# Cross-attention weights divided in SBUF beside the self-attention cells, the second block's mask added there by GpSimd

## The chip, the cores and the metric

The kernel runs on one core of one Trainium2 chip. The metric is the device time of one launch in microseconds (us). The kernel before took 1626.58 us, the median of three runs from 1624.60 to 1629.66.

The engines are named as in the profile: PE (TensorE, matmuls; PEld its weight loads), DVE (VectorE), ACT (ScalarE), POOL (GpSimd), SP (SyncE, whose queue issues most DMAs). PE writes to PSUM, here eight banks of 128 x 512 floats; everything else lies in SBUF.

## What is computed

Two transformer blocks in sequence, all in float32, on `x` of 2 batches x 1024 rows x 256. Each has self-attention with 16 heads of 16, cross-attention to 64 context rows per batch, and a feed-forward. The first block's feed-forward is a mixture of 8 experts, of which each row takes two; the second's is one network. Only the second block's cross-attention has a mask over the context rows. Cut to what matters:

```python
# first block
q = _ln(latents);  x = latents + _mha(q, q, ...)          # self-attention
x = x + _mha(_ln(x), _ln(tokens), ...)                    # cross-attention, no mask
return _fuse_moe(x, ...)                                  # 8 experts, top 2
# second block
attn = softmax(einsum('bhnd,bhmd->bhnm', q, k) * SCALE);  x = x + (...)
q = _heads(layer_norm(x) @ q_w.T)
k = _heads(codebook_embeds @ k_w.T);  v = _heads(codebook_embeds @ v_w.T)
attn = einsum('bhnd,bhmd->bhnm', q, k) * SCALE
bias = (1.0 - mask)[:, None, None, :] * -10000.0
attn = softmax(attn + bias)
x = x + merge(einsum('bhnm,bhmd->bhnd', attn, v)) @ ca_proj_w.T
x = x + gelu(layer_norm(x) @ fc1_w.T + fc1_b) @ fc2_w.T + fc2_b
```

## The kernel before

**Cells.** Self-attention of one block is cut into 128 cells (loop at L959): 2 batches x 2 halves of the queries x 4 groups of 4 heads, times 8 parts of the keys. Eight cells are a head group `h`. A cell does two things. It takes the weights of its own part: four matmuls (L816), four Exp on ACT (L822), and later `product` (L858), which multiplies by the values (L867), copies on ACT (L876 or L879, into `part`) and adds on POOL (L880). And it looks ten cells ahead (`LEAD`) and takes row maxima: four matmuls (L805) and four reductions on DVE (L812). So in the last ten cells of a block, from cell 118 on, there are no maxima left; `maxima[0]` (L965) says whether there are. `helper()` (L314) is POOL while there are, DVE after. Once in eight cells, at cell 6 of a group, `largest` (L708) transposes the maxima (L713), which makes L713 a mark in the trace.

**Stream.** All other work of the block is a set of tasks, Python generators held in a `Stream` (L130). A task yields a positive cost in us when it has issued work, and a zero or negative number when it wants to wait: zero is one cell, -x is x us in cells of 2.9 us, one cell at least. After each cell the loop takes steps of tasks, most urgent and then highest rank first, until the allowance of the cell is used: 2.5 us a cell in the first block, 1.1 in the second, more where due times ask for it (`pace`, L161; L981). Steps without cost use no allowance. When the cells are over, `rest` (L178) issues what is left in order of rank, each task after its waits. All of this order is fixed when the program is made.

**Cross-attention** of a unit of 512 rows n (0 to 3, a batch half each) starts when the unit's self-attention is projected into `x` (`project`, L787). It is three tasks: a norm (`cnorm`), `weigh` (L1103) and `share` (L1273); the norm of unit n waits for the `weigh` of unit n-1, and `weigh` for the `share` of unit n-1. `weigh` works on 2 groups `g` x 4 rows of heads `r`, eight tiles of 128 x 512: query rows on partitions, and 8 stretches (4 query tiles x 2 heads) of 64 context rows along the free dimension. Its steps:

- `scores(g, n)` (L1128): for two tiles, four matmuls each (L1143); in the second block a matmul of one row before each of them puts the mask into the bank (L1134). While there are maxima ACT copies the banks to SBUF (L1154); otherwise `subtract` reads the bank.
- `largest(g, r)` (L1169): on a copied tile, DVE takes the maximum of each stretch (L1163) and POOL subtracts it (L1164).
- `weights_turned(g, n)` (L1173): four transposes on PE (L1179) per tile, and Exp on ACT out of PSUM (L1183) into `pt`.
- `product(g)` (L1189): four matmuls with the values (L1192), and sixteen with a table of ones, `picks` (L1202), that sum the weights; a copy on ACT (L1209), a reciprocal of the sums on DVE (L1211).
- `divided(g)` (L1214): four matmuls that spread the reciprocals over the rows (L1217) and a multiplication on DVE (L1224). For g = 1 it is in `share`, which then projects into `x` (L437).

While there are maxima these steps follow the list at L1232, eleven steps with at least a cell between most of them.

**The first block's end.** After the `share` of a unit, `dispatch_task` (L1306) routes it: norm, router matmuls, many small DVE operations, rows written to `sorted_rows`. `find` and `rows` (L1712, L1735) then say how many slots of 256 rows of one expert can start: after units 0 and 1 one slot, after unit 2 five (`NFULL`, L82). Slots (L1741) are issued only in `rest`. In the second block the feed-forward tasks (L1807) likewise start only in `rest`.

Of the kernel before, what the change touches and what calls it, by code (L numbers as in the profile page):

```python
# [41 lines left out]
F32 = mybir.dt.float32  # L42
# [3 lines left out]
ALU = mybir.AluOpType  # L46
# [4 lines left out]
P = 128  # L51
# [52 lines left out]
NCOL = 139  # L104


O_SUM, O_HEAD = 0, 128

O_ROWS, O_PART = 640, 704
NPICK = 768  # L110

W_O, W_V, W_Q, W_K = 0, 512, 1024, 1536
NSELF = 2048
# [88 lines left out]
def two_blocks(  # L202
# [323 lines left out]
    def self_attention(layer, tail, heads, arrive, extra, when_ready, beside=None):  # L526
# [224 lines left out]
        def side_by_side(parts, dst):  # L751

            i, o = bank()
            j, s = bank()
            for half, part in enumerate(parts):
                nc.tensor.matmul(
                    o[64 * half : 64 * (half + 1), :], lhsT=picks[:, O_ROWS : O_ROWS + 64],
                    rhs=part, start=True, stop=True,
                )
            for half, part in enumerate(parts):  # L760
                for c in range(4):
                    nc.tensor.matmul(
                        s[32 * c : 32 * (c + 1), :P],
                        lhsT=picks[:, O_PART + 32 * half : O_PART + 32 * (half + 1)],
                        rhs=part[:, c * P : (c + 1) * P],
                        start=(half == 0),
                        stop=(half == 1),
                    )
            inv = small.tile([P, P], F32, tag="inv", name=f"inv_{names}", bufs=1)
            nc.vector.reciprocal(inv, s[:, :P])  # L770
            nc.scalar.copy(dst, o)
            free.extend((j, i))
            yield 1.5
            yield -1.6
            i, by = bank()
            for c in range(4):
                nc.tensor.matmul(
                    by[:, c * P : (c + 1) * P],
                    lhsT=picks[:, O_HEAD + c * P : O_HEAD + (c + 1) * P],
                    rhs=inv, start=True, stop=True,  # L780
                )
            nc.vector.tensor_tensor(dst, dst, by, ALU.mult)
            free.append(i)
            yield 0.55
            yield -1.0
# [72 lines left out]
        def product(cells):  # L858

            h = cells[0] // 8  # L860
            b, g = h // 8, h % 4
            for cell in cells:
                stream.until(("values", b, cell % 8 & 6))
            n, o = bank()
            for cell in cells:
                for j in range(4):
                    nc.tensor.matmul(  # L867
                        o[32 * j : 32 * j + VW, :],
                        lhsT=V[b][:, cell % 8, 4 * g + j, :],
                        rhs=exps.pop((cell, j)),  # L870
                        start=(cell == cells[0]),
                        stop=(cell == cells[-1]),
                    )
            if cells[0] % 8 == 0:
                acc[h] = opool.tile([P, 512], F32, tag="acc", name=f"acc_{names}{h}")
                nc.scalar.copy(acc[h], o)  # L876
            else:
                part = opool.tile([P, 512], F32, tag="part", name=f"part_{names}{cells[0]}")
                nc.scalar.copy(part, o)  # L879
                helper().tensor_tensor(acc[h], acc[h], part, ALU.add)  # L880
            free.append(n)
            if cells[-1] % 8 == TB - 1:
                at_cell(cells[-1] + 3, lambda: finish(h, cells[-1] + 3))
# [219 lines left out]
    def weigh(layer, b, pool, w, name, held):  # L1103
# [21 lines left out]
        shape = [P, 4 * 2, SK]  # L1125
        less, pts, whole_scores = {}, {}, set()

        def scores(g, n):  # L1128

            got = [(r, *bank()) for r in (2 * n, 2 * n + 1)]  # L1130
            for t in range(4):
                for r, _, p in got if layer == 1 else ():
                    at = slice(32 * r, 32 * r + 1)
                    nc.tensor.matmul(  # L1134
                        p[:, t * P : (t + 1) * P].rearrange("p (u k) -> p u k", k=SK),
                        lhsT=ones[at, :],
                        rhs=mask_f[at, b * SK : (b + 1) * SK].unsqueeze(1).to_broadcast([1, 2, SK]),
                        start=True,
                        stop=False,
                    )  # L1140
                for r, _, p in got:
                    rows = slice(32 * r, 32 * r + 32)
                    nc.tensor.matmul(  # L1143
                        p[:, t * P : (t + 1) * P],
                        lhsT=q[rows, g, t * P : (t + 1) * P],
                        rhs=kbd[rows, g, b].rearrange("p u k -> p (u k)"),
                        start=(layer == 0),
                        stop=True,
                    )
            for r, i, p in got:  # L1150
                sc = less[g, r] = pool.tile([P, 512], F32, tag="sc", name=f"sc_{name}{g}{r}", bufs=4)
                if maxima[0]:

                    nc.scalar.copy(sc, p)  # L1154
                    whole_scores.add((g, r))
                else:
                    subtract(sc, p, nc.vector, f"{g}{r}")
                free.append(i)

        def subtract(sc, src, engine, tag):  # L1160
# [5 lines left out]
                mx.unsqueeze(2).to_broadcast(shape), ALU.subtract,  # L1166
            )

        def largest(g, r):  # L1169
            if (g, r) in whole_scores:  # L1170
                subtract(less[g, r], less[g, r], nc.gpsimd, f"{g}{r}")

        def weights_turned(g, n):  # L1173

            for r in (2 * n, 2 * n + 1):
                i, p = bank()
                sc = less.pop((g, r))
                for t in range(4):
                    nc.tensor.transpose(  # L1179
                        p[:, t * P : (t + 1) * P], sc[:, t * P : (t + 1) * P], ident  # L1180
                    )
                pt = pts[g, r] = pool.tile([P, 512], F32, tag="p1", name=f"pt_{name}{g}{r}", bufs=4)
                nc.scalar.activation(pt, p, AF.Exp, scale=SCALE)  # L1183
                free.append(i)


        inverse = {}

        def product(g):  # L1189
            i, o = bank()  # L1190
            for r in range(4):
                nc.tensor.matmul(  # L1192
# [7 lines left out]
            for r in range(4):  # L1200
                for c in range(4):
                    nc.tensor.matmul(  # L1202
                        s[32 * c : 32 * (c + 1), :P],
                        lhsT=picks[:, O_SUM + 32 * r : O_SUM + 32 * (r + 1)],
                        rhs=pts[g, r][:, c * P : (c + 1) * P],
                        start=(r == 0),
                        stop=(r == 3),
                    )
            nc.scalar.copy(q[:, g, :], o)  # L1209
            inv = inverse[g] = pool.tile([P, P], F32, tag="inv", name=f"inv_{name}{g}", bufs=2)  # L1210
            nc.vector.reciprocal(inv, s[:, :P])  # L1211
            free.extend((i, j))

        def divided(g):  # L1214
            i, p = bank()
            for c in range(4):
                nc.tensor.matmul(  # L1217
# [6 lines left out]
            nc.vector.tensor_tensor(q[:, g, :], q[:, g, :], p, ALU.mult)  # L1224
            free.append(i)

        held.update(ot=q, divided=divided)
        cost = 1.9 if layer else 1.0
        SC, LA, TU, PR, DI = scores, largest, weights_turned, product, divided
        if maxima[0]:  # L1230

            for now, wait in (  # L1232
                (((SC, 0, 0), (LA, 0, 0)), 0.0),
                (((LA, 0, 1),), 0.0),
                (((SC, 0, 1), (LA, 0, 2)), 0.0),
                (((TU, 0, 0), (LA, 0, 3)), 0.0),
                (((SC, 1, 0), (LA, 1, 0)), 0.0),
                (((TU, 0, 1), (LA, 1, 1)), 0.0),
                (((SC, 1, 1), (LA, 1, 2)), 0.0),
                (((PR, 0), (LA, 1, 3)), -1.5),  # L1240
                (((TU, 1, 0),), None),
                (((DI, 0), (TU, 1, 1)), -1.4),
                (((PR, 1),), None),
            ):
                for step, *args in now:
                    step(*args)
                us = sum({SC: cost, TU: 1.15, PR: 1.1, DI: 0.55}.get(step[0], 0.0) for step in now)
                if us:
                    yield us
                if maxima[0]:  # L1250
                    yield 0.0
                elif wait is not None:
                    yield wait
            return
        for step, *args, wait in (
            (SC, 0, 0, None),
# [1 line left out]
            (TU, 0, 0, None),  # L1258
            (SC, 1, 0, None),
            (TU, 0, 1, -1.3),  # L1260
            (PR, 0, None),
            (SC, 1, 1, None),
            (TU, 1, 0, None),
            (DI, 0, None),
            (TU, 1, 1, -1.6),
            (PR, 1, None),
        ):
            step(*args)
            yield {SC: cost, TU: 1.15, PR: 1.1, DI: 0.55}[step]
            if wait:  # L1270
                yield wait

    def share(w, name, first, held):  # L1273

        yield -2.6
        held["divided"](1)
        yield 0.55
        yield -1.2
        for t0 in range(0, 4, 2):
            yield from project_task(held["ot"], w, first + t0, t0, 2)  # L1280
# [732 lines left out]
def _layout(inputs):  # L2013
# [81 lines left out]
    cols[:E, C_RB] = l0["router_b"]  # L2095

    picks = np.zeros((P, NPICK), f32)
    for r in range(4):
        for u in range(2):
            for c in range(4):  # L2100
                picks[SK * u : SK * (u + 1), O_SUM + 32 * r + 8 * c + 2 * r + u] = 1.0
    for j in range(4):
        for d in range(DH):
            picks[32 * j + d, O_ROWS + DH * j + d] = 1.0
# [49 lines left out]
```

## Time and profile before

The profiled execution took 1611.58 us; its span on the core, from first to last instruction, is 1609.8 us at a mean granted PE clock of 0.988.

| what | number |
|---|---|
| median of the runs | 1626.58 us |
| profiled execution, span | 1611.58 us, 1609.8 us |
| cells of the first block, last matmul | to about 588 us |
| slots of the experts | 597 to about 941 us |
| cells of the second block, last matmul | to about 1451 us |
| last cross-attention projected | 1523 us |
| L1134, mask matmuls | 256 instructions, 27.5 us of PE busy |
| L1202 and L1217, sums and their spreading | 512 and 128 instructions, 17.5 and 17.6 us |
| POOL subtractions (L1164) | 38 of 64 tiles |

A matmul of float32 appears as two instructions, so 512 matmul records of L1202 are 8 units x 32 matmuls. Matmuls on different rows or columns of the array overlap in time, so busy times of a group are more than what it takes from the cells around it. A line of the groups reads: line, engine, operation, output from inputs, shape, count; then busy time in us and the mean of one in ns; then idle time just before and what ended it. A line of the timeline reads: start in us, length in us, engine, line, operation, count. A line of busy times reads: stretch, its length, then busy time and instructions of PE, PEld, DVE, ACT and POOL, the granted clock, the DMA share and GB/s.

### The profile page before, as it was taken

The numbers are of one execution on the slowest core, as the hardware profiler recorded it, in microseconds if no ns is written. First come the engines' busy times: TensorE is split into PE (matmuls) and PEld (weight loads), VectorE is DVE, ScalarE is ACT, GpSimd is POOL, SyncE is SP. The second block draws the span as 40 slices with busy tenths as digits, with TensorE's granted clock in tenths as the row PEclk, the third lists the DMA queues.
The fourth block names the chain that finished last, engine by engine and source line by source line (L and its number), as shares of the span: only waits on it lengthen the run. The fifth ranks groups of instructions, "written<-read, shape, count | busy, mean of one in ns | idle before, by whom it ended". The sixth has DMA issues, their size and how long they took to land. (4 is left out here: it accounts for less than half of the span.)

```text
span 1609.8 us, 28322 instructions
## 1 busy us (share of the span) xinstructions
PE 1574.8 (98%) x10710; PEld 876.0 (54%) x10710; DVE 982.6 (61%) x2094; ACT 914.7 (57%) x1770; POOL 410.9 (26%) x546
## 2 busy tenths in 40 slices
PE   7999999999999999999999999999999999999998
PEld 3433444444544447888888653344344445446766
DVE  5797766677679747511114458876777777854400
ACT  3487767666765665332223337876776676674321
POOL 2233423135235203311112033411222322311000
PEclk9899999999999999999999999999999999999999
DMA  5334311101000115386556320101010002000000
GB/s 158 114 134 169 138 27 31 28 25 47 15 21 34 54 50 196 105 278 205 187 188 216 92 78 23 35 21 24 31 38 17 22 14 84 20 9 21 14 13 26
DMA packets 55751, 121.07 MB, mean 75 GB/s; under 512 B 12218, under 2 KB 26428, under 8 KB 55228
## 3 DMA queue, kind: packets, MB, share of 16 engines
q1 hardware_dynamic: 51772, 109.07, 20.9%
q0 software_dynamic: 3456, 9.51, 1.6%
q8 instruction: 86, 1.41, 0.4%
q10 hardware_dynamic: 384, 0.66, 0.2%
q14 instruction: 53, 0.43, 0.1%
HBM read 71.68 MB, written 38.88 MB: 69 GB/s over the span
## 5 line engine op out<-in xcount | busy, mean ns | idle before, releaser
L812 DVE TENSOR_REDUCE mx_s<-banks 128x1 f32<-128x512 f32 x1024 | 634.0, 681 | 209.5 <-PE banks L805 207.2
L822 ACT ACTIVATE pt_s<-banks 128x512 f32<-128x512 f32 x1024 | 532.8, 609 | 157.1 <-PE banks L805 123.8
L805 PE MATMUL banks<-KS,QS 16*128 16x512 f32 x2048 | 535.1, 631 | 2.9 <-DVE count L1446 1.4
L816 PE MATMUL banks<-qb_s,KS 32*128 32x512 f32 x2048 | 516.8, 622 | 6.9 <-DVE qb_s L715 3.6
L880 POOL TENSOR_TENSOR acc_s<-acc_s,part_s 128x512 f32<-128x512 f32 x141 | 179.4, 1272 | 434.5 <-ACT part_s L879 433.9
L816 PEld LDWEIGHTS banks<-qb_s,KS 32*128 32x128 f32 x2048 | 180.8, 187 | 178.7 <-DVE mx_s L812 106.3
L867 PE MATMUL banks<-pt_s,v_s 128*20 128x512 f32 x2048 | 262.7, 604 | 1.5 <-DVE mx_s L812 1.0
L805 PEld LDWEIGHTS banks<-KS,QS 16*128 16x128 f32 x2048 | 200.3, 186 | 71.7 <-issue 34.2
L867 PEld LDWEIGHTS banks<-pt_s,v_s 128*20 128x20 f32 x2048 | 43.1, 98 | 185.8 <-ACT pt_s L822 130.4
L1686 PE MATMUL banks<-w_slot,h_s 128*128 128x256 f32 x640 | 143.1, 380 | 0.0
L1686 PEld LDWEIGHTS banks<-w_slot,h_s 128*128 128x128 f32 x640 | 120.6, 190 | 19.7 <-DVE mx_s L812 1.5
L879 ACT COPY part_s<-banks 128x512 f32<-128x512 f32 x155 | 92.7, 598 | 62.3 <-PE banks L867 52.6
L1695 DVE SCALAR_TENSOR_TENSOR ys<-banks,gate,b 128x256 f32<-128x256 f32 x40 | 19.3, 482 | 163.0 <-PE banks L1686 161.8
L1662 ACT ACTIVATE h_s<-banks,w_slot 128x256 f32<-128x256 f32 x104 | 43.7, 471 | 111.1 <-issue 64.0
L1656 PE MATMUL banks<-xsT,w_slot 128*128 128x256 f32 x416 | 95.4, 381 | 0.7 <-ACT xsT L376 0.7
L1701 POOL DMA_INDIRECT results<-ys,to x40 | 38.8, 970 | 223.0 <-DVE ys L1695 180.5
L1656 PEld LDWEIGHTS banks<-xsT,w_slot 128*128 128x128 f32 x416 | 77.4, 190 | 14.9 <-DVE mx_s L812 2.3
L1164 POOL TENSOR_TENSOR sc_c<-sc_c,mx_c 128x512 f32<-128x512 f32 x38 | 40.0, 1053 | 97.6 <-DVE mx_c L1163 97.5
L1819 ACT ACTIVATE h_f<-banks,w_ff 128x512 f32<-128x512 f32 x32 | 22.0, 687 | 73.9 <-PE banks L1816 73.9
L635 PE MATMUL banks<-xT_s,w_att 128*128 128x512 f32 x128 | 63.9, 635 | 0.0
L1828 PE MATMUL banks<-w_ff,h_f 128*128 128x256 f32 x256 | 57.3, 380 | 0.0
L1662 ACT ACTIVATE h_s<-banks,spare 128x256 f32<-128x256 f32 x56 | 23.4, 471 | 58.7 <-issue 30.4
(272 smaller groups left out, 1640.2 us busy)
## 6 DMA issues: line engine op xcount, KB each, us to landing
w_slot<-in_ff_w_dram SPq DMA_DIRECT2D x40, 576.0 KB
sorted_rows<-fill SPq DMA_DIRECT2D x36, 520.0 KB
w_slot<-in_ff_w_dram SPq DMA_DIRECT2D x26, 514.0 KB
whole<-acc_s SPq DMA_DIRECT2D x30, 256.0 KB
spare<-in_ff_w_dram SPq DMA_DIRECT2D x14, 514.0 KB
xs<-sorted_rows SPq DMA_DIRECT2D x20, 260.0 KB
y<-results SPq DMA_DIRECT2D x16, 256.0 KB
QS<-stq_s SPq DMA_DIRECT2D x124, 32.0 KB
```

The source lines that it names most:

```text
L635: nc.tensor.matmul(p, lhsT=w[:, at + k * D + pair * P : at + k * D + (pair + 1) * P], rhs=xT[b][:, k, blk * 512 : (blk + 1) * 512], start= ...
L805: nc.tensor.matmul(sc, lhsT=QS[h % 4][r, qc * P : (qc + 1) * P], rhs=K[r, kh * 512 : (kh + 1) * 512], start=True, stop=True,)
L812: return i, lambda: nc.vector.tensor_reduce(mx[h][:, qc, j, kh : kh + 1], sc, AX.X, ALU.max)
L816: nc.tensor.matmul(sc, lhsT=K[r, n * P : (n + 1) * P], rhs=QB[h][r, :], start=True, stop=True)
L822: nc.scalar.activation(pt, sc, AF.Exp, scale=SCALE)
L867: nc.tensor.matmul(o[32 * j : 32 * j + VW, :], lhsT=V[b][:, cell % 8, 4 * g + j, :], rhs=exps.pop((cell, j)), start=(cell == cells[0]), st ...
L879: nc.scalar.copy(part, o)
L880: helper().tensor_tensor(acc[h], acc[h], part, ALU.add)
L1656: nc.tensor.matmul(ph[:, n, :], lhsT=w[:, at : at + P], rhs=xT[:, k, :], start=(k == 0), stop=(k == 1),)
L1662: nc.scalar.activation(h1[:, f, :], ph[:, n, :], AF.Gelu, bias=w[:, W_B1 + f : W_B1 + f + 1])
L1686: nc.tensor.matmul(py, lhsT=h1[:, f, h * P : (h + 1) * P], rhs=w[:, f * D : (f + 1) * D], start=(f == 0), stop=(f == 7),)
L1828: nc.tensor.matmul(py[:, n, :], lhsT=h1[:, f, t * P : (t + 1) * P], rhs=w2[:, f * D : (f + 1) * D], start=(f == 0), stop=(f == 7),)
```

## The change

A `weigh` that starts while there are maxima (`whole`) no longer sums and divides after the product. It takes Exp in SBUF (`exponentials`), sums each stretch of 64 on DVE, takes 8 reciprocals per row and lets `helper()` multiply (`divided`); the turned tiles are then only copied by ACT, and `product` is the four matmuls and the copy. In the second block its scores have no mask matmuls: POOL adds the mask to the copied tiles (`mask`). The steps follow a computed list of 19 (first block) or 21 (second block) steps, one cell each at least. `share` then has no division and starts with its second wait. A `weigh` that starts without maxima keeps the old steps, renamed `undivided` and `division`. The planner's costs follow. The table for the sums becomes one window that is shifted, `inv` moves to the buffers of `xn`, and `part` has three buffers instead of two.

```diff
-                part = opool.tile([P, 512], F32, tag="part", name=f"part_{names}{cells[0]}")
+                part = opool.tile([P, 512], F32, tag="part", name=f"part_{names}{cells[0]}", bufs=3)
...
+        whole = maxima[0]
+
         def scores(g, n):
             got = [(r, *bank()) for r in (2 * n, 2 * n + 1)]
+            masked = layer == 1 and not maxima[0]
             for t in range(4):
-                for r, _, p in got if layer == 1 else ():
+                for r, _, p in got if masked else ():
...
-                        start=(layer == 0),
+                        start=not masked,
...
+        def mask(g, r):
+            if (g, r) in whole_scores:
+                sc = less[g, r].rearrange("p (c k) -> p c k", k=SK)
+                row = mask_f[:, b * SK : (b + 1) * SK].unsqueeze(1).to_broadcast(shape)
+                nc.gpsimd.tensor_tensor(sc, sc, row, ALU.add)
+
+        def exponentials(g, r):
+            nc.scalar.activation(less[g, r], less[g, r], AF.Exp, scale=SCALE)
+
+        def divided(g, r):
+            sc = less[g, r].rearrange("p (c k) -> p c k", k=SK)
+            sm = pool.tile([P, 8], F32, tag="smc", name=f"sm_{name}{g}{r}", bufs=4)
+            nc.vector.tensor_reduce(sm, sc, AX.X, ALU.add)
+            nc.vector.reciprocal(sm, sm)
+            helper().tensor_tensor(sc, sc, sm.unsqueeze(2).to_broadcast(shape), ALU.mult)
...
-                nc.scalar.activation(pt, p, AF.Exp, scale=SCALE)
+                if whole:
+                    nc.scalar.copy(pt, p)
+                else:
+                    nc.scalar.activation(pt, p, AF.Exp, scale=SCALE)
...
         def product(g):
...
+            nc.scalar.copy(q[:, g, :], o)
+            free.append(i)
+        def undivided(g):
...
-        def divided(g):
+        def division(g):
...
+        costs = {
+            scores: 1.9 if layer and not maxima[0] else 1.0, weights_turned: 1.15, product: 0.55,
+            undivided: 1.1, division: 0.55,
+        }
+        if whole:
+            m = layer
+            cells = [[] for _ in range(19 + 2 * m)]
+            for k in range(8):
+                g, r = divmod(k, 4)
+                at = k + (4 + m) * g
+                if r % 2 == 0:
+                    cells[at].append((SC, g, r // 2))
+                    cells[at + 7 + m].append((TU, g, r // 2))
+                if m:
+                    cells[at].append((MA, g, r))
+                cells[at + m].append((LA, g, r))
+                cells[at + m + 2].append((EX, g, r))
+                cells[at + m + 3].append((DI, g, r))
+            for g in range(2):
+                cells[11 + m + (7 + m) * g].append((PR, g))
+            for now in cells:
+                for step, *args in now:
+                    step(*args)
+                us = sum(costs.get(step, 0.0) for step, *_ in now)
+                if us:
+                    yield us
+                if now is not cells[-1]:
+                    yield 0.0 if maxima[0] else -1.5
...
     def share(w, name, first, held):
-        yield -2.6
-        held["divided"](1)
-        yield 0.55
+        if held["division"]:
+            yield -2.6
+            held["division"](1)
+            yield 0.55
         yield -1.2
```

More of the change, by code (lines that the diff above doesn't have):

```diff
@@ L104 @@
 NCOL = 139
-O_SUM, O_HEAD = 0, 128
-O_ROWS, O_PART = 640, 704
-NPICK = 768
+O_SUM, O_HEAD = 512, 0
+O_ROWS, O_PART = 552, 616
+NPICK = 680
 W_O, W_V, W_Q, W_K = 0, 512, 1024, 1536
@@ L768, in side_by_side @@
                     )
-            inv = small.tile([P, P], F32, tag="inv", name=f"inv_{names}", bufs=1)
+            inv = small.tile([P, D], F32, tag="xn", name=f"inv_{names}", bufs=6)[:, :P]
             nc.vector.reciprocal(inv, s[:, :P])
@@ L1182, in weights_turned, with product @@
                 pt = pts[g, r] = pool.tile([P, 512], F32, tag="p1", name=f"pt_{name}{g}{r}", bufs=4)
-                nc.scalar.activation(pt, p, AF.Exp, scale=SCALE)
+                if whole:
+                    nc.scalar.copy(pt, p)
+                else:
+                    nc.scalar.activation(pt, p, AF.Exp, scale=SCALE)
                 free.append(i)
+        def product(g):
+            i, o = bank()
+            for r in range(4):
+                nc.tensor.matmul(
+                    o[32 * r : 32 * (r + 1), :],
+                    lhsT=vbd[:, b, 4 * g + r, :],
+                    rhs=pts[g, r],
+                    start=True,
+                    stop=True,
+                )
+            nc.scalar.copy(q[:, g, :], o)
+            free.append(i)
         inverse = {}
-        def product(g):
+        def undivided(g):
             i, o = bank()
@@ L1203, in product @@
                         s[32 * c : 32 * (c + 1), :P],
-                        lhsT=picks[:, O_SUM + 32 * r : O_SUM + 32 * (r + 1)],
+                        lhsT=picks[:, O_SUM + 6 - 2 * r : O_SUM + 38 - 2 * r],
                         rhs=pts[g, r][:, c * P : (c + 1) * P],
@@ L1209, in product @@
             nc.scalar.copy(q[:, g, :], o)
-            inv = inverse[g] = pool.tile([P, P], F32, tag="inv", name=f"inv_{name}{g}", bufs=2)
+            inv = inverse[g] = small.tile([P, D], F32, tag="xn", name=f"inv_{name}{g}", bufs=6)[:, :P]
             nc.vector.reciprocal(inv, s[:, :P])
             free.extend((i, j))
-        def divided(g):
+        def division(g):
             i, p = bank()
@@ L1225, in divided @@
             free.append(i)
[L1227 to L1244, printed above, removed]
+        held.update(ot=q, division=None if whole else division)
+        costs = {
+            scores: 1.9 if layer and not maxima[0] else 1.0, weights_turned: 1.15, product: 0.55,
+            undivided: 1.1, division: 0.55,
+        }
+        SC, MA, LA, EX, DI, TU, PR = (
+            scores, mask, largest, exponentials, divided, weights_turned, product
+        )
+        if whole:
[15 more added lines that the diff above has]
+            for now in cells:
                 for step, *args in now:
                     step(*args)
-                us = sum({SC: cost, TU: 1.15, PR: 1.1, DI: 0.55}.get(step[0], 0.0) for step in now)
+                us = sum(costs.get(step, 0.0) for step, *_ in now)
                 if us:
                     yield us
[L1250 to L1253, printed above, removed]
+                if now is not cells[-1]:
+                    yield 0.0 if maxima[0] else -1.5
             return
@@ L1260, in weigh @@
             (TU, 0, 1, -1.3),
-            (PR, 0, None),
+            (undivided, 0, None),
             (SC, 1, 1, None),
             (TU, 1, 0, None),
-            (DI, 0, None),
+            (division, 0, None),
             (TU, 1, 1, -1.6),
-            (PR, 1, None),
+            (undivided, 1, None),
         ):
             step(*args)
-            yield {SC: cost, TU: 1.15, PR: 1.1, DI: 0.55}[step]
+            yield costs[step]
             if wait:
@@ L2097, in _layout @@
     picks = np.zeros((P, NPICK), f32)
[L2098 to L2101, printed above, removed]
+    for u in range(2):
+        for c in range(4):
+            picks[SK * u : SK * (u + 1), O_SUM + 6 + 8 * c + u] = 1.0
     for j in range(4):
```

## The prediction

> **What bounds the kernel now.** I read the page's busy times and slices first, then busy time by stretch, then the groups of instructions of the cross-attention, then the timeline.
>
> ```profile
> PE 1574.8 (98%) x10710; PEld 876.0 (54%) x10710; DVE 982.6 (61%) x2094; ACT 914.7 (57%) x1770; POOL 410.9 (26%) x546
> ...
> PE   7999999999999999999999999999999999999998
> ...
> DVE  5797766677679747511114458876777777854400
> ACT  3487767666765665332223337876776676674321
> ```
>
> PE is covered in nearly every slice, with DVE and ACT at six to eight tenths beside it in the two stretches of cells. The Trainium skill, page "Perfetto Trace Analysis", section "Identifying the Most-Contended Engine", warns that matmul busy time is a poor measure because matmuls are pipelined. So I tested PE by what a cell costs with and without other PE work. Busy times by stretch (sum, then each engine):
>
> ```profile
> 110.20:134.36 24.16, 24.16 (x200) 8.17 (x196) 21.91 (x40) 20.51 (x41) 9.09 (x19) 1.00 0.40 136
> 265.40:304.10 38.70, 38.70 (x325) 19.04 (x321) 25.83 (x43) 27.55 (x53) 10.34 (x10) 1.00 0.14 28
> 477.37:512.16 34.79, 32.87 (x228) 14.06 (x224) 28.49 (x75) 21.04 (x41) 11.85 (x22) 1.00 0.05 16
> 553.30:588.40 35.10, 34.93 (x313) 16.45 (x309) 15.62 (x32) 26.69 (x53) 1.04 (x1) 1.00 0.00 1
> 588.40:641.50 53.10, 49.68 (x363) 37.03 (x362) 38.21 (x147) 26.71 (x51) 12.71 (x13) 0.97 0.50 171
> ```
>
> The first two are eight cells each. Matmuls other than L805, L816 and L867 cover 0.7 us of the first and 14.7 us of the second (by the timeline): 14.5 us longer for 14.0 us of extra PE work. Over the 28 such stretches of both blocks a straight line gives 24.3 us + 1.06 x extra PE time; with DVE's and ACT's extra time added to the fit these cost 0.25 and 0.27 us per us. A bare cell is 3.0 us. PE sets the pace, but DVE is at 21.9 of 24.2 us even in bare cells. In the third stretch, full of the router's small DVE operations, DVE is at 28.5 of 34.8 and the cells are longer than their PE work: DVE is the next bound.
>
> **What the skill says.** "SBUF — State Buffer", section "Who interferes with whom": GpSimd shares a port pair with DVE; a DVE instruction with two SBUF inputs contends with a GpSimd instruction that reads SBUF, tensor_reduce never does. The trace agrees: L1357 (two SBUF inputs, usually 0.19 us) took 1.14 us beside a GpSimd add, while the reduces of L1163 stay at 0.63 to 0.69 us. The new DVE reduces and reciprocals are of the free kind, so the added GpSimd work slows only the router's and norms' small operations.
>
> **The change part by part.** The present prices, by shape, and pieces of the timeline (start, length):
>
> ```profile
> L1134 PE MATMUL banks<-mask_i,ones 1*128 1x128 f32 x256 | 27.5, 281 | 0.0
> L1202 PE MATMUL banks<-pt_c,picks 128*32 128x128 f32 x512 | 17.5, 273 | 0.0
> L1217 PE MATMUL banks<-inv_c,picks 128*128 128x128 f32 x128 | 17.6, 280 | 0.3 <-DVE inv_c L1211 0.2 <-DVE mx_s L812 0.2
> L1211 DVE RECIPROCAL inv_c<-banks 128x128 f32<-128x128 f32 x16 | 15.3, 958 | 25.3 <-PE banks L1202 25.3
> L1224 DVE TENSOR_TENSOR q_c<-q_c,banks 128x512 f32<-128x512 f32 x16 | 10.9, 682 | 12.8 <-PE banks L1217 12.8
> L1163 DVE TENSOR_REDUCE mx_c<-sc_c 128x8 f32<-128x512 f32 x38 | 25.6, 673 | 14.7 <-ACT sc_c L1154 14.7
> L1164 POOL TENSOR_TENSOR sc_c<-sc_c,mx_c 128x512 f32<-128x512 f32 x38 | 40.0, 1053 | 97.6 <-DVE mx_c L1163 97.5
> L1183 ACT ACTIVATE pt_c<-banks 128x512 f32<-128x512 f32 x64 | 35.6, 612 | 20.6 <-PE banks L1179 19.9 <-ACT pt_c L1183 0.6
> ```
> ```profile
> 258.13 1.05 PE L1143 MATMUL banks<-kbd,q_c 32*128 32x128 f32 x14
> 258.91 0.70 PE L805 MATMUL banks<-KS,QS 16*128 16x512 f32 x2
> ...
> 490.06 1.29 POOL L880 TENSOR_TENSOR acc_s<-acc_s,part_s 128x512 f32<-128x512 f32 x1 [10.51 <-ACT part_s L879]
> 490.27 1.14 DVE L1357 TENSOR_TENSOR hot_m<-hot_m,desc 128x32 f32<-128x32 f32 x1
> ...
> 1177.19 0.49 PE L1134 MATMUL banks<-mask_i,ones 1*128 1x128 f32 x3
> 1178.98 0.70 PE L805 MATMUL banks<-KS,QS 16*128 16x512 f32 x2
> ```
>
> Only tasks whose scores begin while maxima are still taken get the new form. By the scores' times these are three of the first block (scores from 258, 389 and 534 us; maxima end near 553) and two of the second (1177 and 1311; the third begins at 1431, after maxima end near 1415).
>
> PE, per task. One sums step runs from 295.8 to 296.8 (1.0 us), two are 2.0; one division step from 304.6 to 305.5 (0.9), two are 1.8. Gone: 3.8 us. In the second block scores with masks hold PE from 1177.19 to 1178.98 (1.8 us), those of the first from 258.13 to 258.91 (0.8): four steps give another 4.0, so 7.8. All five: 3 x 3.8 + 2 x 7.8 = 27.0 us. That is the whole possible gain.
>
> DVE, per task. Gone: 2 x 0.96 + 2 x 0.68 = 3.3. New: 8 sums at 0.67 (L1163's row) and 8 reciprocals of 128x8; the nearest rows are 0.18 (128x4, L1409) and 0.34 (128x32, L497), I take 0.2. 7.0 in all, net +3.7. ACT: 8 Exp more at about 0.6, net +4.8, as the copies after the turns cost what the Exp there cost (0.60 against 0.61). GpSimd: 8 multiplications at 1.05 = 8.4; in the second block 8 mask adds at 1.05 to 1.27 (L429, an add with the same broadcast), so 17 to 19. It is busy 10 of 39 us in such cells, and the third `part` buffer lets ACT run ahead of it.
>
> Give-back. The fit gives 3.7 x 0.25 + 4.8 x 0.27 = 2.2 us per task. The other bound is denser: maximum, sum and reciprocal come in cells where this task has no PE work, so four cells in a row hold 2.48 + 0.87 of DVE or more, one of them 2.48 + 1.55: 14.1 us of DVE against 11.8 for four bare cells. Twice per task that is 4.6, near 5 with ACT. I take 3; the ends are 2.2 and 5.
>
> New waits. Exp waits on ACT for GpSimd's subtraction two cells before, the sum on DVE for an Exp one cell before, the turns on PE for a multiplication three cells before; behind each stand the next cell's reductions, Exps and matmuls. With GpSimd at most two such operations and one add per cell (3.4 us of about 4) these hold, unless GpSimd stands before a DMA (it waited up to 11.2 us for `by_s` before L508). I count nothing, with 3 us per block as the bad end.
>
> First two tasks of the first block: 3.8 - 3 = 0.8 each, -1.6. They last 19 cells, not 11. Their successors wait for the projected self-attention rows anyway (481.7 us), so the chain isn't later, only the router's work beside it.
>
> Second block: 7.8 - 3 = 4.8 each, -9.6. The first task took 19 cells as its costs exceeded the allowance of 1.1 us a cell; 21 steps with 9.7 us of cost take some 22 to 25. The second ends 5 to 10 cells later, near cell 118, and the next starts in the tail. There 2.8 of 4 blocks of feed-forward remain when the last cross-attention ends (1523 us), so lateness is filled. I charge 1 us: -8.6.
>
> Third task of the first block. It starts at cell 113; its sixteenth step falls on cell 128, so two turns, a product and the projection (5.4 us of PE) pass the last cell. Before, its projection ran at 575.6, 12.8 us before the cells ended at 588.4. By the planner's costs and waits (1.15 + 1.5 + 0.55 + 1.2 + 4.0) it now ends about 9 us after, and the router's task behind it, which already ran its statistics in those cells, has 5.8 of waits more to its normalisation: 15.5 after the end instead of 3 (591.4), so 12.5 later. Slots 1 to 4 need the rows it sorts (two units guarantee 2 x 2 x 512 - 8 x 255 = 8 rows, one slot); their first matmul came at 641.5, 53.1 after the cells. Meanwhile PE has the other work, 45 to 59 us of it. The last twelve cells shrink by 3 us (PE loses 7, but ACT, at 26.7 of 35.1, gains 2.4); the fourth task's division and projection, which ran after 641.5, now come before (4.5). Sum: -3 + 12.5 - 4.5 = +5, between 0 and +15.
>
> Total: -1.6 - 8.6 + 5 = -5.2 us on the profiled run's 1611.6 (span 1609.8 and 1.8 around it): 1606.4, a ratio of 0.9968. The profiled run is 15 us below the median of 1626.58, so I apply the ratio: 1621.
>
> The moved tiles (`inv` among the six `xn`, `picks` 88 columns shorter) I cost at nothing: a reciprocal's tile is read within 8 us, and picks arrives long before use. If that cover went, a norm would wait 1 us or so.
>
> **Rivals.**
> Full gain: PE alone counts and the tail fills: -27.0, 1599.6. For it, the slope of 1.06; against it, DVE at nine tenths in bare cells. Chance 0.20.
> Late rows (slower): the third task ends 21 us later relative to the cells, the whole distance, and the router's DVE chain (37 us from 586 to 623) then meets the fourth task's maxima and subtractions (13 us of DVE), 5 more. The tail is -3 + 21 - 4.5 + 5 = +18.5, the total +8.3: 1635. It decides once slot 1's first matmul is over 76 us after the last cell. For it: slot 0 is the only slot at hand. Chance 0.27.
> DVE and ACT take PE's place: 5 us back per task: +2.4 - 5.6 + 1 + 5 = +2.8, 1629. Chance 0.10.
> The third task falls back to the old form, pushed past the end of maxima by the later router: the tail stays, -1.6 - 8.6 = -10.2, 1616. Chance 0.05.
> Forecast: 0.38, own range 1614 to 1629.
>
> **How the numbers follow.** What a measurement here can tell from no change is about 0.3%, 4.9 us. Faster: full gain 0.20, fallback 0.05, 0.22 of the forecast: 0.47. Same: 0.13 of the forecast and 0.08 of the fourth case: 0.21. Slower: late rows 0.27, 0.05 of the others: 0.32. The range, 1602 to 1636, takes in the unknown costs and most of the outer cases.
>
> **What would show it.** Right: L1134's count falls from 256 to 128, the sums' from 512 to 192; heads of the second block with a task 1.5 us shorter each; slot 1 about 65 us after the first block's last cell, with some 7 us of PE idle before it. Wrong: PE waiting in cells for ACT's new Exp or for DVE behind GpSimd; five tasks not in the new form; no idle before slot 1.

## The result and the profile after

Beside runs of the kernel before on the same chip (median 1628.1 us) the changed kernel took 1616.4 us, the median of four runs: a ratio of 0.9935, interval 0.9918 to 0.9953. A second measurement, on one of the three chips of the experiments, gave 1610.2 us and 0.9957 (0.9943 to 0.9971). The ratios and intervals are estimated from the single runs and are not the quotients of the medians (0.9928 and 0.9969 here). The forecast was 0.9968. So the kernel is 0.4 to 0.65% faster.

The profiled execution of after took 1614.6 us, 3 us more than that of before in the table above. The experiments' three chips ran the kernel before at 1612 to 1615 us (medians), where its first profile (1611.6) also lies, and not at 1626 to 1628. A different chip would explain this, but the record names none for the first measurement. Nor is it a common factor: before took 0.8 to 1.0% more there, after (1616.4 against 1610.2) only 0.4%. Times from different chips are compared below as ratios to the kernel before on the same chip, and checked against the stretches of the traces. A difference of two ratios is turned into us by 1612; its uncertainty is worked out from the two intervals.

The totals and slices of after, to hold against those of before:

```profile
PE 1560.5 (97%) x10182; PEld 853.7 (53%) x10182; DVE 1013.8 (63%) x2178; ACT 939.3 (58%) x1821; POOL 472.2 (29%) x589
...
PE   7999999999999888899999999999999999999998
...
DVE  5788776877878856511114458876777878845400
```

PE has 528 instructions fewer and is busy for 14.3 us less; DVE has 31 us more. New are the eights in PE's slices 14 to 17: holes about the end of the first block's cells and behind it. The groups of after by shape, new and shrunk ones:

```profile
L1139 PE MATMUL banks<-mask_i,ones 1*128 1x128 f32 x128 | 12.9, 282 | 0.0
L1240 PE MATMUL banks<-pt_c,picks 128*32 128x128 f32 x192 | 8.3, 280 | 3.1 <-issue 3.1
L1191 DVE TENSOR_REDUCE sm_c<-sc_c 128x8 f32<-128x512 f32 x40 | 26.8, 670 | 0.0
L1192 DVE RECIPROCAL sm_c<-sm_c 128x8 f32<-128x8 f32 x40 | 8.1, 203 | 1.4
L1185 ACT ACTIVATE sc_c<-sc_c 128x512 f32<-128x512 f32 x40 | 26.0, 651 | 0.0
L1193 POOL TENSOR_TENSOR sc_c<-sc_c,sm_c 128x512 f32<-128x512 f32 x33 | 34.9, 1057 | 13.9 <-DVE sm_c L1192 13.8
```

Forty tiles are five tasks: the change does what it says, at about the prices taken (0.67, 0.2, 0.65 and 1.06 us; 0.67, 0.2, 0.6 and 1.05 were forecast). GpSimd takes 33 of the 40 multiplications, DVE the seven that come after the maxima. The stretches that the prediction showed of before, here of after (stretch, length, then PE, PEld, DVE, ACT and POOL busy, clock, DMA share, GB/s):

```profile
110.20:134.70 24.50, 24.37 (x201) 8.37 (x197) 21.97 (x40) 20.52 (x41) 9.06 (x19) 1.00 0.43 143
260.05:293.91 33.86, 33.86 (x252) 14.36 (x249) 25.93 (x47) 27.07 (x53) 14.97 (x14) 1.00 0.16 33
467.73:498.65 30.92, 30.31 (x224) 13.43 (x221) 28.40 (x58) 21.80 (x42) 13.05 (x34) 1.00 0.03 10
537.66:568.90 31.24, 28.62 (x217) 10.88 (x214) 23.93 (x61) 27.38 (x55) 3.60 (x4) 0.99 0.16 52
568.90:644.30 75.40, 63.53 (x427) 46.42 (x427) 45.39 (x154) 26.05 (x52) 13.84 (x14) 0.95 0.29 95
```

Bare cells are about as long as before (24.5 us for eight, 24.2 before). The stretches with cross-attention shrank by 3.9 to 4.8 us each (38.70, 34.79 and 35.10 before). The last line ends with slot 1's first matmul with its weights (L1701): 75.4 us after the last cell, 53.1 before, with 11.9 us of idle PE in it. Both halves of the forecast are there, and both are larger than forecast.

### The profile page after: what moved, and what is told of

Read it like the earlier page. It is cut to its first block, busy times and chain, and to the rows that moved or that the text cites. A ratio compares the mean times of both kernels' runs of the same rounds, so it can differ in the third digit from the quotient of the medians.

```text
span 1612.8 us, 27523 instructions
## 1 busy us (share of the span) xinstructions
PE 1560.5 (97%) x10182; PEld 853.7 (53%) x10182; DVE 1013.8 (63%) x2178; ACT 939.3 (58%) x1821; POOL 472.2 (29%) x589
## 5 line engine op out<-in xcount | busy, mean ns | idle before, releaser
L881 POOL TENSOR_TENSOR acc_s<-acc_s,part_s 128x512 f32<-128x512 f32 x151 | 191.6, 1269 | 370.3 <-ACT part_s L880 369.2
L880 ACT COPY part_s<-banks 128x512 f32<-128x512 f32 x166 | 100.3, 605 | 45.8 <-PE banks L868 41.3
L1701 PE MATMUL banks<-xsT,w_slot 128*128 128x256 f32 x416 | 96.2, 383 | 0.9 <-ACT xsT L377 0.9
L1701 PEld LDWEIGHTS banks<-xsT,w_slot 128*128 128x128 f32 x416 | 78.0, 191 | 15.4 <-DVE mx_s L813 2.3
L1861 PE MATMUL banks<-hT_f,w_ff 128*128 128x512 f32 x128 | 56.8, 594 | 0.0
```

Source lines behind the costliest of these rows:

```text
L1701: nc.tensor.matmul(ph[:, n, :], lhsT=w[:, at : at + P], rhs=xT[:, k, :], start=(k == 0), stop=(k == 1),)
L1861: nc.tensor.matmul(ph, lhsT=w1[:, at : at + P], rhs=hT[:, k, :], start=(k == 0), stop=(k == 1))
```

## The experiments

Diffs are against the changed kernel. Where a task keeps the old form, its old list of eleven steps is put back, with its masks and costs. Stretches of eight cells, between marks L714 (L713 before), repeat mostly to 0.1 us from run to run and chip to chip where the order and the granted clock are the same; in what follows they locate what the timed ratios weigh.

**The kernel before, again.**

> The kernel before, unchanged, for a second profile of it. Its first profiled execution (1611.6 us) was 15 us below the median of its runs. Theory A (that execution was a quick one): a new profile lies within 5 us of the timed runs, near 1626, with the surplus spread over the cells (first block's cells near 595 us, the second's near 515) and slot 1's first matmul again near 53 us after the last cell. Theory B (the profile of this kernel is always quicker than its timed runs): near 1612 again.

Median 1612.6 us, ratio 1.0004 (0.9996 to 1.0012); profiled at 1609.2. Both theories fall: profile and timed runs agree here. The stages are those of the first profile, but for 1.8 us in the stretch from 134 us and 0.7 in the one before the last maxima.

**The third task, and the second block's second, in the old form.**

```diff
-        whole = maxima[0]
+        whole = maxima[0] and name in ('c00', 'c01', 'c10', 'c11')      # third_old
+        whole = maxima[0] and name in ('c00', 'c01', 'c02', 'c10')      # last_old
+        whole = maxima[0] and name in ('c00', 'c01', 'c10')      # third_last_old
```

> The changed kernel, but the third cross-attention task of the first block keeps the old form (eleven steps, Exp after the turns, sums and division by matmuls). Theory T (the late third task costs the tail): slot 1's first matmul falls back from 75 to about 55 to 60 us after the last cell; PE has 3.8 us more to do; the sum is 6 to 12 us faster than the changed kernel, near 1607. Rival R (PE is full in the tail anyway, the lateness is filled with other work): 2 to 4 us slower than the changed kernel, near 1619.

> The changed kernel, but the second of the two new-form tasks of the second block keeps the old form with its mask matmuls. Theory T (lateness of the second task costs the tail after the cells too): the last cross-attention is projected 15 us nearer to the last cell and the time falls 3 to 8 us below the changed kernel, near 1611. Rival R (feed-forward fills that tail): PE gets its 7.8 us back and the time is 5 to 8 us above the changed kernel, near 1623.

> Both of these at once, so that only the first two tasks of the first block and the first of the second have the new form. If the effects of the two are independent, their sum: with theory T for the first and R for the second near 1613; with T for both near 1602; with R for both near 1626, about the time of the kernel before.

Measured: 0.9865 (0.9844 to 0.9885), 0.9955 (0.9936 to 0.9973), 0.9886 (0.9870 to 0.9903). The third task's new form costs 14.8 +- 4.0 us against the second measurement of after, and 11.1 +- 4.0 between the last two, which ran on one chip: theory T. For the second block's second task neither expectation came: its new form gains 3.4 +- 4.2 us between third_last_old and third_old and loses 0.3 +- 3.7 between last_old and the second measurement of after. That is nothing clear of noise. In last_old the last cross-attention is projected 78.3 us after the last cell (90.7 in the second profile of after), so theory T's lateness is there; it costs about what the task saves. Within the noise the two effects add up.

What happens in the tail, from the waits of PE between the last cell and some 75 to 90 us later, first after, then third_old (waits in all, times, longest, in us):

```profile
PE banks L370 <- DVE xd_m L1364: 6.5, 1, 6.5
PE banks L370 <- DVE xn_c L358: 3.6, 2, 1.9
PE banks L1240 <- issue: 3.1, 6, 1.1
PE banks L370 <- DMA ctx<-in_ctx_dram: 2.2, 1, 2.2
PE banks L1437 <- DVE chosen_m L1417: 1.2, 1, 1.2
```
```profile
PE banks L757 <- DVE acc_s L881: 2.1, 1, 2.1
PE banks L370 <- DMA ctx<-in_ctx_dram: 0.9, 1, 0.9
PE banks L1201 <- DVE sc_c L1169: 0.9, 2, 0.6
PE banks L1463 <- DVE before_m L1455: 0.3, 1, 0.3
```

In third_old matmuls of slot 0 stand before the fourth norm (xn_c) and the third unit's chosen_m, and those of slot 1 before the fourth unit's xd_m. With the third task late less work stands before them, and PE waits for the small DVE operations. The longest wait, for xd_m, lies just behind slot 1's start (644 to 649 us in the second profile of after). Counted from the last product of the cells, slot 1's first instruction on PE (the turning of its rows, 1 to 3 us ahead of the matmul counted above) comes after 50.1 us in third_old, 50.3 in the kernel before and 70.2 in the second profile of after. These three tails, of before_again, third_old and after_again:

```profile
586.14:636.40 50.26, 46.83 (x316) 34.64 (x316) 36.36 (x133) 24.18 (x45) 12.68 (x13) 0.97 0.47 159
```
```profile
578.40:628.50 50.10, 45.70 (x316) 33.59 (x316) 36.35 (x133) 24.27 (x45) 12.68 (x13) 1.00 0.49 163
```
```profile
569.08:639.28 70.20, 60.90 (x418) 44.60 (x419) 45.70 (x155) 25.33 (x50) 13.87 (x15) 0.95 0.26 90
```

Much of the added PE time in the tail is work that came later before. The net cost shows from the last mark but one of the first block, near 500 us, to the first mark of the second, third_old, then after_again:

```profile
502.49:930.73 428.24, 419.82 (x2386) 320.19 (x2383) 196.62 (x642) 173.65 (x363) 86.51 (x88) 1.00 0.45 151
498.81:942.62 443.81, 424.12 (x2307) 319.99 (x2304) 206.49 (x662) 174.38 (x368) 87.96 (x89) 0.98 0.43 146
```

With the third task in the new form this is 15.6 us longer: PE is idle for 11.3 us more, and busy for 4.3 us more with about 80 instructions fewer. The clock explains the latter: it is at half for 20.5 us here (6.8 each from 531, 613 and 648 us), for 3.4 us in third_old, which is 8.5 us of lost clock.

**The changed kernel again, and only the first two tasks in the new form.**

```diff
+        whole = maxima[0] and name in ('c00', 'c01')      # first_two_new
```

> The changed kernel unchanged, so that it stands beside the other variants on one chip. The ratio to the kernel before was 0.9935 on another chip. Theory C (that chip was about 1% slower for every kernel, the ratio carries over): 0.9935 +- 0.002 here, with slot 1's first matmul again 65 to 70 us after the last cell against 42 in the kernel before. Rival: the late third task costs a different amount from run to run, and the ratio falls outside 0.990 to 0.997.

> Only the first two tasks of the first block have the new form; the whole second block is as before. Compared with the variant that also has the first task of the second block in the new form (ratio 0.9886) this prices that one task. By the prediction's sums it is worth 4.8 us: 0.9916. If PE time alone counts, 7.8 us: 0.9934. If most of what the cells gain is given back after them, 0 to 2 us: 0.9886 to 0.9898. And the first two tasks by themselves: by the prediction 1.6 us of gain (0.999), by PE time alone 7.6 (0.995), by the profiles taken so far about 10 (0.994).

0.9957 (0.9943 to 0.9971): nearest to theory C, which gave 0.9955 and 70 us as its upper ends (slot 1 came 70.2 us after the last cell). First_two_new: 0.9885 (0.9865 to 0.9905). So the first task of the second block is worth 0.2 +- 4.2 us, and both new-form tasks of that block together 3.2 +- 4.6 (third_old against first_two_new), where the prediction had 8.6. The surprise is the first block, priced by the next pair.

**The third buffer of part.**

```diff
+        whole = maxima[0] and name in ()      # none_new
```
```diff
-                part = opool.tile([P, 512], F32, tag="part", name=f"part_{names}{cells[0]}", bufs=3)
+                part = opool.tile([P, 512], F32, tag="part", name=f"part_{names}{cells[0]}")      # after_two_parts
```

> The changed kernel with no task in the new form: every engine has the same instructions in the same order as in the kernel before; what is left of the change is the third buffer of part, the reciprocals in xn's buffers and the shorter table. Theory P (the gain of the first block is the third buffer's, which the prediction counted at nothing; the new form itself gains nothing there): about the ratio of the variant with only the first two tasks in the new form, 0.9885, within 0.003, and the stretch of eight cells from 134 to 165 us is 27.2 us long, not 31. Rival D (the gain is the division's, whose PE work goes): only that stretch is shorter, 4 to 6 us in all, 0.996 to 0.9975; the stretches of the first task in the new form (38.7 and 33.8 us before, 33.9 and 29.1 after) stay as before.

> The changed kernel with two buffers for part, as before; the order on every engine is that of the changed kernel. Its ratios were 0.9935 and 0.9957. Theory P: it loses some 18 us and is slower than the kernel before, 1.004 to 1.010. Rival D: it loses 4 to 6 us, 0.997 to 1.000.

None_new: 0.9972 (0.9960 to 0.9984), after_two_parts: 1.0015 (1.0003 to 1.0028). Rival D for the first: what is left without the new form gains 4.5 +- 1.9 us, not 18; theory P falls. After_two_parts lies between the two expectations, 9.4 +- 3.0 us above after_again, which ran on another chip. Its profile is only 5.0 us longer than that of after_again, so this is not clearly more than none_new's 4.5. Without its third buffer the whole change would have made the kernel no faster, by the ratio slightly slower. The place shows in before_again (start, length, engine):

```profile
135.19 1.27 POOL L508 TENSOR_TENSOR ot_s<-ot_s,by_s 128x512 f32<-128x512 f32 x1 [7.25 <-DMA by_s<-turns]
136.42 3.94 POOL L880 TENSOR_TENSOR acc_s<-acc_s,part_s 128x512 f32<-128x512 f32 x3
137.72 0.59 ACT L879 COPY part_s<-banks 128x512 f32<-128x512 f32 x1 [2.93 <-POOL acc_s L880]
138.35 1.17 PE L805 MATMUL banks<-KS,QS 16*128 16x512 f32 x4 [1.24 <-ACT part_s L879]
```
```profile
138.00:140.00 2.00, 1.65 (x8) 0.46 (x12) 0.45 (x1) 2.00 (x5) 1.92 (x2) 0.83 0.95 385
140.00:142.00 2.00, 2.00 (x12) 0.52 (x8) 0.84 (x2) 0.78 (x2) 0.37 (x1) 0.50 0.25 102
142.00:144.00 2.00, 2.00 (x20) 0.64 (x16) 0.77 (x2) 0.93 (x3) 1.26 (x1) 0.82 0.00 0
```

GpSimd waited 7.25 us for a DMA, three additions piled up, ACT waited 2.93 us for a buffer of part, and PE 1.24 for ACT. Then (second view, busy times by two us) PE's granted clock fell to half for 3.4 us, as the three clocks add up to. So 1.24 us of waiting made the stretch 3.9 us longer: 1.2 of waiting, 1.7 of lost clock, and 0.9 that were not traced. The stretch takes 31.0 us there and 31.2 in after_two_parts, 27.2 in none_new and every variant with three buffers. In the first profile it is 32.8; there the clock stayed at half for 6.8 us. The other stretches of none_new are as before within 0.6 us, so the gain is the buffer's and not that of the moved tiles.

That leaves the first two tasks: first_two_new against none_new is -14.0 +- 3.8 us. The first two stretches of the first task, none_new, then first_two_new:

```profile
259.93:298.69 38.76, 38.76 (x325) 19.04 (x321) 25.84 (x43) 27.56 (x53) 10.34 (x10) 1.00 0.14 28
298.69:332.45 33.76, 33.76 (x280) 16.32 (x276) 25.82 (x48) 22.06 (x42) 8.33 (x10) 1.00 0.09 26
```
```profile
257.96:291.81 33.85, 33.85 (x252) 14.35 (x248) 25.93 (x47) 27.08 (x53) 14.97 (x14) 1.00 0.16 33
291.81:320.88 29.07, 29.07 (x240) 12.45 (x236) 24.73 (x45) 25.24 (x50) 15.77 (x14) 1.00 0.09 30
```

The clock is full in both. DVE's busy time is the same or less here, because the longer task puts the rest off: these two are 9.6 us shorter, the two after them 6.0 longer. The second of those, none_new, then first_two_new:

```profile
367.76:404.23 36.47, 36.23 (x273) 18.40 (x273) 28.13 (x62) 25.56 (x51) 20.05 (x19) 1.00 0.17 53
```
```profile
357.51:398.62 41.11, 39.56 (x264) 16.63 (x264) 31.86 (x73) 28.45 (x56) 14.11 (x13) 0.92 0.07 21
```

The router's DVE operations, put off, meet the maxima here. PE waits 2.2 us for maxima (0.7 in none_new), the clock falls to half for 6.8 us, and of the 4.6 us more 3.4 are lost clock. None_new loses as much in the stretch before the last maxima, where first_two_new loses none, so the sum is not the clock's doing. Over all eight stretches to the last maxima the sum is 12.3 us less (10.3 in third_old), for 160 matmul instructions removed and none moved out in sum: 5.2 to 6.2 us a task, net of all that DVE and ACT got.

**The masks.**

```diff
-            masked = layer == 1 and not maxima[0]
+            masked = layer == 1      # third_old_pe_masks, on top of third_old
...
-                if m:
-                    cells[at].append((MA, g, r))
```

> The variant with the third task of the first block in the old form (ratio 0.9865), and in the second block the two new-form tasks take their masks from the PE matmuls again, with no mask additions on GpSimd; the list of steps keeps its 21 places and its costs, so the order is the same. It prices the mask's move. By the prediction 4.0 us of PE a task: 8 us slower, 0.991. Rival (one-row matmuls run beside the others, and GpSimd's adds delay the chain of a tile): 0 to 2 us slower or even faster, 0.985 to 0.988.

0.9899 (0.9883 to 0.9916): 5.5 +- 4.2 us slower than third_old, between the two expectations. The eight stretches with these tasks grow by 6.4 us for 128 mask matmuls, against the 8.0 that the prediction counted. So the mask's move pays. Set against first_two_new, division alone in the second block is +2.3 +- 4.2 us: nothing gained.

Masks_alone has no task in the new form, but GpSimd's additions in a list of thirteen steps:

```diff
+        whole = maxima[0] and name in ()      # masks_alone
+                (((SC, 0, 0), (MA, 0, 0), (MA, 0, 1)), 0.0),
+                (((LA, 0, 0),), 0.0),
+                (((SC, 0, 1), (MA, 0, 2), (LA, 0, 1)), 0.0),
...
```

> No task in the new form (old sums and division by matmuls everywhere, third buffer of part kept), but in the second block GpSimd adds the mask to the copied scores, in a list of thirteen steps. Theory P with the mask's measured price (5.5 us for two tasks): that much under the kernel with no task in the new form, 0.984 to 0.987. If the longer list gives it back after the cells: no different from it, 0.988 to 0.990.

0.9946 (0.9926 to 0.9966), 4.2 +- 3.8 us under none_new: the price again, if barely clear of noise, but not the 0.984 to 0.987 expected, since that rested on theory P.

**A doubled sum.**

```diff
             nc.vector.tensor_reduce(sm, sc, AX.X, ALU.add)
+            nc.vector.tensor_reduce(sm, sc, AX.X, ALU.add)      # on top of third_old
```

> The variant with the third task of the first block in the old form (ratio 0.9865), with the sum of every tile taken twice on DVE in the four new-form tasks: 32 reductions more of about 0.67 us, 21.4 us of DVE. If DVE time costs what the fit over the kernel before gave (0.25 us per us): 5.4 us slower, 0.990. If DVE is the bound in the cells with sums: 15 to 21 us slower, 0.996 to 1.000. If DVE has room in these cells: 0 to 1.5 us, 0.987.

0.9983 (0.9966 to 1.0000): 19.0 +- 4.3 us slower for 21.4 us of DVE; DVE is the bound in the cells with sums. One such stretch, third_old, then with the doubled sum:

```profile
1233.51:1262.19 28.68, 28.68 (x232) 11.29 (x229) 24.64 (x45) 25.04 (x49) 18.29 (x16) 1.00 0.09 29
```
```profile
1242.18:1273.39 31.21, 30.34 (x232) 12.01 (x229) 27.31 (x49) 25.38 (x49) 19.41 (x17) 1.00 0.09 27
```

Four sums more are 2.67 us of DVE and 2.53 us of time, with PE busy nearly throughout in both: busy PE here doesn't mean that PE sets the pace. In the sixteen stretches of the four tasks the doubled sums cost 16.3 us of 21.4, or 0.76 us per us; 3.4 us of it are lost clock (at half for 13.7 us near 400, 6.8 in third_old), without which it is 0.6.

**The third task, two steps a cell.**

```diff
+            if name == "c02":      # third_two_a_cell
+                cells = [a + b for a, b in zip(cells[::2], cells[1::2] + [[]])]
             for now in cells:
```

> The changed kernel, with the nineteen steps of the third task of the first block taken two to a cell, so that it lasts ten cells and keeps the new form. If it is the task's length that costs the tail: slot 1's first matmul comes back to about 45 us after the last cell, as with the old form, and the ratio is near that of the old form, 0.985 to 0.989. Rival (sums, maxima and multiplications packed into half the cells stall PE): the stretches of its cells grow by 5 us or more and the ratio stays at 0.990 to 0.995.

Half of each. The tail is back: slot 1 comes 50.1 us after the last cell. But the ratio is 0.9949 (0.9931 to 0.9968), no different from after. The stretch before the last maxima, third_two_a_cell, then after_again:

```profile
498.45:545.27 46.82, 43.34 (x286) 19.88 (x283) 36.93 (x86) 30.42 (x59) 24.45 (x23) 0.89 0.12 41
```
```profile
498.81:537.83 39.02, 37.12 (x254) 15.98 (x251) 33.22 (x77) 26.29 (x52) 16.79 (x16) 0.92 0.12 42
```

7.8 us longer, the next up to the last cell 7.1 more: the longest waits of PE, 2.8 and 3.1 us, are for the multiplications and the router's DVE, and the clock falls to 0.89. So it is the task's length that costs the tail's 20 us, but packing it pays 15 of them in the cells.

## Why the forecast held, step by step

The total was right in sign and within its range, but by errors that cancel. Chained from run to run, the sum is -4.5 (buffer) - 14.0 (first two tasks) - 3.2 (second block) + 14.8 (third task) = -6.9 us, which is after_again by construction; forecast -5.2. That the total came within 2 us of the forecast is luck.

- **Third buffer of part: the prediction mentioned it and counted nothing.** It gained 4.5 +- 1.9 us alone and 9.4 +- 3.0 within the change. The prediction even named the wait (GpSimd before a DMA, up to 11.2 us for `by_s`) but only as a danger to the new steps, not as a loss that the old kernel already had.
- **First two tasks, "0.8 each, -1.6": mis-sized, -14.0 +- 3.8 (stretches: -10.3 to -12.3).** Two terms. PE at 3.8 a task, from single pieces of the timeline, is below the groups' own busy times: L1202 and L1217 are 35.1 us over eight tasks, 4.4 each. And the give-back of 3 us a task didn't appear as a net loss. DVE isn't free, as the doubled sum shows; at 0.6 to 0.76 per us its net 3.7 us would cost 2.2 to 2.8. By this estimate the removed steps were worth some 7 to 9 us a task, up to twice their busy time. What made them so dear was not isolated: the reciprocal of 0.96 us between them and the second bank that they held are candidates, no run separated them. The fit's prices (1.06 for PE, 0.25 for DVE) were no firm ground either: over all 30 stretches the same fit gives 0.93 for PE alone and, with the others added, 0.80 for PE and 0.45 for DVE. And the sum over dense cells took four bare cells as 11.8 us; by the lines shown (24.16 for eight) they are 12.1.
- **Masks, "four steps give another 4.0": right in kind,** 5.5 +- 4.2 (6.4 in the stretches) of 8.0 for two tasks. What GpSimd's additions cost by themselves was not separated.
- **Second block, "lateness is filled, I charge 1 us": wrong.** The cells gain as expected and more: its eight stretches with tasks are 15.7 us shorter in third_old than in none_new, 2 each and not 1.5. But the tail takes it back. The last stretch of cells and the tail, none_new, then third_old:

```profile
1408.49:1444.50 36.01, 33.93 (x300) 15.70 (x300) 15.59 (x30) 28.54 (x57) 6.27 (x16) 1.00 0.03 9
1444.50:1517.50 73.00, 71.90 (x573) 52.85 (x566) 35.88 (x77) 25.11 (x40) 5.49 (x16) 1.00 0.06 20
1517.50:1603.50 86.00, 81.70 (x292) 54.36 (x290) 9.09 (x19) 17.73 (x27) 5.41 (x16) 1.00 0.06 19
```
```profile
1389.36:1418.50 29.14, 28.66 (x201) 10.62 (x197) 14.31 (x45) 25.21 (x51) 3.24 (x5) 1.00 0.03 10
1418.50:1509.20 90.70, 86.20 (x706) 63.32 (x706) 47.39 (x96) 36.67 (x56) 11.54 (x29) 0.98 0.05 16
1509.20:1597.00 87.80, 83.54 (x297) 55.30 (x295) 9.15 (x19) 18.42 (x28) 5.41 (x16) 1.00 0.05 18
```

  Moving 99 matmul instructions out of the last cells made these 6.9 us shorter; 138 more in the tail (the other 39 come from earlier stretches) made it 19.5 us longer, 16.1 of it PE's busy time and 3.4 idle. In the last cells ACT is at 25 to 28 us of 29 to 36 and work on PE lies partly beside it; in the tail PE is busy nearly throughout and pays in full. The prediction asked only whether other work fills the tail, not what the moved work cost at either place.
- **Third task, "+5, between 0 and +15": the mechanism was right, the size at the upper end,** +11.1 and +14.8. Slot 1 came 75.4 us after the last cell, not 65 (the rival of late rows put its point at 76), with 11.9 us of PE idle, not 7. The term of 12.5 us for the later router task (its own parts, 9 and 5.8 and 3 taken off, give 11.8) left out that the router's DVE chain then runs bare, and that PE's clock falls in the holes: 11.3 us of idle PE and 8.5 of lost clock, as shown above.
- **New waits in the cells at nothing: right only for the new tiles.** The new sums (L1191) waited for nothing (0.0 in the groups of after), took 0.63 to 0.68 us in all forty places beside the busier GpSimd, and no wait of PE stands against the new Exp. But the shifted order brought the router's DVE work and the maxima together, and there PE waited (2.2 us in the stretch shown, with 3.4 us of lost clock in first_two_new and 5.1 in after). For the first block the prediction's bad end of 3 us was nearer.

Third_old is the fastest of all: 1593.6 us, 1.35% under the kernel before; first_two_new (1596.4, 0.9885) and third_last_old (1594.8, 0.9886) can't be told from it.

## What to carry to other kernels

Ask of a longer task not only what it costs but which work it pushes past the end of the stage: matmuls were cheaper beside cells in which ACT was nearly full than in the tail. When a change carries a small buffer along, price the wait that the old kernel has there, and run it alone. Look at the granted clock beside every hole of PE. Where several engines are near nine tenths, a busy engine need not be the bound; a doubled operation tells.

## What was not expected of the hardware

Short waits can cost PE more than their length. The Trainium skill, page "TensorE: Matmul & The Clock Gate", section "What's actually happening", has the clock at half after an idle window of about 3.4 us, the window running free of the kernel. Here a wait of 1.24 us was enough: the clock was 0.50 from 140 to 142 us, and matmuls of 0.59 us took 1.22. In the tail of after_again it is 0.57, 0.50 and 0.79 after waits at 610 to 613:

```profile
574.00:577.00 3.00, 0.88 (x9) 0.72 (x8) 1.08 (x4) 1.08 (x3) 0.00 (x0) 1.00 0.62 208
...
610.00:613.00 3.00, 1.93 (x24) 1.57 (x22) 2.67 (x15) 1.59 (x4) 0.00 (x0) 1.00 0.00 0
613.00:616.00 3.00, 2.63 (x8) 2.23 (x9) 2.81 (x8) 0.00 (x0) 0.00 (x0) 0.57 0.00 0
616.00:619.00 3.00, 3.00 (x13) 1.41 (x15) 2.32 (x12) 0.20 (x1) 0.25 (x1) 0.50 0.00 0
619.00:622.00 3.00, 3.00 (x53) 2.04 (x45) 0.97 (x3) 0.59 (x1) 2.39 (x3) 0.79 0.24 88
```

But 2.1 us without work at 574 to 577 were followed by none. The measurements decide against a fixed length of the gap; what else the gate looks at, no run here shows. The length of the half clock does fit the page's window: the shown clocks add up to 3.4 us at half in the first place and 6.8 in the second, and inside all fourteen profiles, their ends apart, it comes in multiples of 3.4 us, each 1.7 us of lost clock.
